# The last stage of a two-layer GNN and expert kernel: half 1's tokens scattered to places group by group, its expert results added into the output, the last tile finished beside the first expert sets

## The chip, the cores and the metric

The kernel runs on one core of one Trainium2 chip. Its time is device time in microseconds (us), of one launch that computes the whole reference. The median of several runs is the figure that is compared; the profile comes from one profiled execution of its own time.

The core's engines work side by side, each through its own instructions in order: PE (matrix multiply; PEld is its weight load), DVE and ACT (vector and activation work), POOL (here mostly transfers with indices) and SP (here only transfers). Transfers run on 16 DMA engines. Data in the on-chip memory lie in 128 partitions; "128x256" is 128 partitions of 256 elements.

## The reference, cut to what matters

There are N = 3125 tokens of D = 256 features and 50000 edges. Two layers follow each other, and each adds a graph part and an expert part to x. The second layer is the one that the change touches:

```
# layer 2, graph part (gnn): count-weighted sums over edges
t1    = feat @ W1                            # feat = layernorm(x)
msg   = t1[src] + feat[src] * feat[dst] @ W2
msg   = msg / (sqrt(deg[src]) * sqrt(deg[dst]))
embed = where(in_cnt > 0, t1 + segment_sum(msg, dst), 0) + b
embed = leaky_relu(embed, 0.01)
x     = x + embed / max(norm(embed), 1e-12)

# layer 2, expert part (ffn), tokens = layernorm(x)
probs = softmax(tokens @ router_w.T)         # 8 experts
rw, re = top_k(probs, 2); rw = rw / rw.sum()
out = tokens
for e in range(8):
    h = gelu(tokens @ w1[e] + b1[e])         # 256 -> 256
    out = out + combine[:, e] * (h @ w2[e] + b2[e])
x = x + out
```

Every token goes to its two best experts, and the result is x plus the normed tokens plus the two weighted expert outputs.

## The kernel before

**Tiles, halves, sets.** The 3125 tokens are 25 tiles of 128; the last one (tile 24) has 53. `X` holds all of x on the chip. The expert part works on two halves, tiles 0 to 13 and 14 to 24 (`HALVES`). For each half there are eight sets, one for each expert, with a fixed room of 4 tiles of 128 places in half 0 and 3 in half 1 (`UNITS`); tokens that don't fit would go to extra sets behind a branch at the end, which is not taken in the profiled execution. So sets 0 to 7 are half 0's, sets 8 to 15 half 1's.

**Aggregation.** `to_the_end` runs the end of the program. PE sums, for two tiles at a time, products of the edge counts (`at`) and the neighbours' parts (L1503). Behind the sums of each tile stands `finish_tile`: the products with the summed neighbours (L1395), four transposes (L1399), a copy by ACT (L1401), the dense matmuls (`y`, L1404), leaky ReLU and the square sum (L1406 to L1409). When a group of five tiles is complete (0 to 4, 5 to 9, 10 to 13, 14 to 18, 19 to 23, and 24 alone), `unit` divides by the norm and adds into `X` (L1417), and `score` takes the layer norm (L479 to L486, `xn`), transposes it (L815), multiplies by the router (L820) and, for half 1, writes `xn` to a table in memory, `xtab`. POOL adds `xn` to `X` (L1421).

**Routing.** `route_steps` ranks the scores of a half (L567 to L574), counts the tokens of each expert, gives each token a place, computes the two weights, and `list_steps` (L737 to L765 and beyond) turns this into lists: which token stands in which place (`take`), and which row of the result table it goes to (`put`). Half 0's routing runs in the aggregation; then `dispatch` has POOL scatter its rows (L1475) to their places in a table, two scatters for each tile. Half 1's routing (`beside_third`) runs in steps beside the first sets: `experts` has fixed points between its matmuls (`slot`), and each takes one step from the work beside it.

**Experts.** For a set, the rows come by one load of SP for half 0 (L904, places are in order in the table), and by three POOL gathers for half 1 (L909, by the list). PE transposes them (L925) and DVE copies them to `xs` (L926). PE multiplies by the first weights into `big` (L949), ACT applies GELU into `hid` (L953), PE multiplies by the second weights (`y`, L962), DVE adds the bias (L967; ten `y` buffers), and POOL scatters the 128 rows to the result table `ytab` (L968). Weights are loaded three sets ahead by SP (L844 to L852). The order on each engine is the order in which the program was written out (`manual_schedule`).

**The end.** Results of half 0 are read back beside half 1's sets (`beside_fourth`): SP loads two tiles of `ytab` (L985), DVE adds weight times result into `X` (L998), SP stores the tiles to `out` (L1015). After the last set `combine_all` does the same for half 1, with six loads in flight, the last tile's 53 rows by a load (L989) and a store (L1018) of their own. Then the branch on extra sets closes the program (L1549).

Of the kernel before, what the change touches and what calls it, by code (L numbers as in the profile page):

```python
# [40 lines left out]
UNITS = (4, 3)  # L41
FIXED = [NE * u for u in UNITS]
# [26 lines left out]
def groups(n, size, first=0):  # L69
    return [(a, min(a + size, n)) for a in range(first, n, size)]  # L70

# [18 lines left out]
def gnn_ffn_kernel(ctx: ExitStack, tc: tile.TileContext, x, src_a, src_d, dst_d, dst_row,  # L90
# [134 lines left out]
    def clear(ytab):  # L225
        for _ in clear_steps(ytab):
            pass

    def tables(h, layer, by_place=False):

        rows = (FIXED[h] + XS * SX if by_place else HALVES[h][1] - HALVES[h][0]) * P
        return (dram.tile([rows, D], F32, name=f"xtab{layer}{h}{int(by_place)}"),
                dram.tile([2 * tokens(h), D], F32, name=f"ytab{layer}{h}{int(by_place)}"))
# [343 lines left out]
    class Routed:  # L577
# [5 lines left out]
        def __init__(self, by_place=False, part=T):  # L583
            self.by_place = by_place
            self.part = part
            self.done = False
            self.lists = {}
# [26 lines left out]
    def route(*args):  # L614
        r = Routed()
        for _ in route_steps(r, *args):
            pass
        return r

    def route_steps(r, rp, h, pl, layer, sc=None):  # L620
# [87 lines left out]
        yield from list_steps(r, rp, h, layer, 0, FIXED[h])  # L708
# [17 lines left out]
        r.weight_x = keep.tile([P, 2, n], F32, tag=f"weightx{layer}{h}", name="weight_x")  # L726
        nc.vector.scalar_tensor_tensor(r.weight_x, r.at, FIXED[h] * P - 0.5, r.weight, OP.is_gt, OP.mult)
        yield

    def list_steps(r, rp, h, layer, c0, c1):  # L730

# [13 lines left out]
        pt = bank([P, 2, nl], F32, "sa", 1)  # L745
# [7 lines left out]
        for i, a, b in parts:  # L753
# [6 lines left out]
            col = rp.tile([P, min(r.part, n), 2, nl], BF16, name="col", bufs=2)  # L760
            nc.vector.tensor_tensor(in_pairs(col[:, :m, 1, :]), pairs(cb[:, i, a:b], nl),
                                    in_pairs(iota_b[:, None, :nl].to_broadcast([P, m, nl])), OP.is_equal)
            nc.vector.tensor_tensor(in_pairs(col[:, :m, 0, :]), in_pairs(col[:, :m, 1, :]),
# [20 lines left out]
        none = rp.tile([P, nl], F32, name="no")  # L784
        nc.vector.tensor_scalar(none, pt[:, 0, :], 0.5, float(1 << 20), OP.is_lt, OP.mult)
        nc.vector.tensor_tensor(put, which, none, OP.max)
        r.lists[c0, c1] = (take, put)
# [14 lines left out]
    def score(sp, h, t0, t1, pl, Wt, xtab, also=None, kept=None, queue=nc.sync):  # L802
# [3 lines left out]
        xn = kept if kept is not None else sp.tile([P, 5, D], F32, name="xn5")  # L806
        for t in range(t0, t1):
            normed(xn[:, t - t0, :], X[:, t, :], mv, t - t0)
            if also:
                also(t, xn[:, t - t0, :])  # L810
        for a, b in groups(t1 - t0, 2):
# [5 lines left out]
            nc.scalar.copy(hT[:, :b - a], pt[:, :b - a])  # L817
            for i in range(a, b):
# [3 lines left out]
        if kept is None:  # L822
            queue.dma_start(out=xtab[(t0 - first) * P:(t1 - first) * P, :].rearrange("(t p) d -> p t d", p=P),
                            in_=xn[:, :t1 - t0, :])

    def alone(dma, table, fresh=False):
# [3 lines left out]
        tc.add_to_no_dep_group(group, dma.ins)  # L830

# [23 lines left out]
    def experts(fp, sets, routed, tabs, weights, nh, act, beside=(), fresh=False, early=0, loaded=None,  # L855
# [60 lines left out]
        def turn(k):  # L916
            if k < len(sets):
# [3 lines left out]
                turned[k] = fp.tile([P, KD, max(UNITS) * P], F32, name="xs", bufs=1)  # L921
# [8 lines left out]
        with tc.manual_schedule(engines=ENGINES):  # L930
            for _ in range(early):
                slot()
# [7 lines left out]
            for k, (h, e, x) in enumerate(sets):  # L940
# [4 lines left out]
                hid = fp.tile([P, nh, max(UNITS) * P], F32, name="hid", bufs=2 if nh == 2 else 1)  # L945
# [13 lines left out]
                for j in range(n):  # L959
                    py = bank([P, D], F32, "y")  # L960
                    for c in range(nh):
# [6 lines left out]
                    alone(nc.gpsimd.indirect_dma_start(  # L968
                        out=tabs[h][1], out_offset=bass.IndirectOffsetOnAxis(ap=routed[h].column(c0 + j)[1], axis=0),
                        in_=y, in_offset=None, bounds_check=2 * tokens(h) - 1, oob_is_err=False), tabs[h][1], fresh)  # L970
# [30 lines left out]
    def combine_all(fp, h, r, ytab, over, then=lambda t0, t1: None, bufs=2):  # L1001
        spans = groups(HALVES[h][1], 2, HALVES[h][0])
        ahead = []
        for i, (t0, t1) in enumerate(spans):
            while len(ahead) < min(bufs, len(spans) - i):
                ahead.append(results(fp, h, ytab, *spans[i + len(ahead)], bufs))
            y2 = ahead.pop(0)
            for t in range(t0, t1):
                combine(h, r.weight_x if over else r.weight, y2, t0, t)
            then(t0, t1)  # L1010

    def store(t0, t1):
        whole = min(t1, T - 1)
        if whole > t0:
            nc.sync.dma_start(out=out[t0 * P:whole * P, :].rearrange("(t p) d -> p t d", p=P),  # L1015
                              in_=X[:, t0:whole, :])
        if t1 == T:
            nc.sync.dma_start(out=out[(T - 1) * P:, :], in_=X[:LAST, T - 1, :])  # L1018
# [152 lines left out]
    tabs2 = [tables(h, 2, not h) for h in range(2)]  # L1171
    routed1 = [None, Routed()]
    into = keep.tile([P, GW, W], F32)
    mv2 = keep.tile([P, T, 2], F32)
    with tc.tile_pool(name="ffn", bufs=2, reuse_waits="tile") as fp:
# [134 lines left out]
        def beside_first():  # L1310
# [7 lines left out]
            with tc.tile_pool(name="onehots", bufs=2, reuse_waits="tile") as hp:  # L1318
                yield from total_in(hp, into)
                clears = [c for table in (tabs2[0][0], tabs2[0][1], tabs2[1][1]) for c in (clear_steps(table),)]  # L1320
# [71 lines left out]
    def dense(gp, t, s, feat, some, emb, sq):  # L1392
# [3 lines left out]
        nc.vector.scalar_tensor_tensor(both[:, 1, :], s, deg[:, t:t + 1], feat, OP.mult, OP.mult)  # L1396
        pt = bank([P, 2 * KD, P], F32, "tr")
# [3 lines left out]
        nc.scalar.copy(hT, pt)  # L1401
        po = bank([P, D], F32, "y")
        for k in range(2 * KD):
            nc.tensor.matmul(po, hT[:, k, :], (hW1t if k < KD else hW2t)[:, k % KD, :],  # L1404
                             start=(k == 0), stop=(k == 2 * KD - 1))
        nc.vector.scalar_tensor_tensor(emb, po, some, hbt, OP.mult, OP.add)  # L1406
        nc.vector.scalar_tensor_tensor(emb, emb, 0.01, emb, OP.mult, OP.max)
        junk = gp.tile([P, D], F32, name="junk", bufs=1)
        nc.scalar.activation(junk, emb, AF.Square, accum_out=sq)  # L1409

    def unit(emb, sq, t0, t1):
        n = t1 - t0
        nc.scalar.activation(sq[:, :n], sq[:, :n], AF.Sqrt)
        nc.vector.tensor_scalar(sq[:, :n], sq[:, :n], 1e-12, None, OP.max)
# [7 lines left out]

    def to_the_end():


        routed2 = [Routed(True, 5), Routed()]
        with tc.tile_pool(name="ahead", bufs=6, side="right", reuse_waits="tile") as ap, \
                tc.tile_pool(name="prod", bufs=1, reuse_waits="tile") as gp:
            at = {}

            def load(t):
                if t % 8 < 6:
                    at[t] = ap.tile([P, T, P], BF16, name="at")
                else:
                    at[t] = gp.tile([P, T, P], BF16, name="at2", bufs=2)
# [10 lines left out]
            def finish_tile(sp, t, s):  # L1446
# [7 lines left out]
                dense(gp, t, s, feat, some_in[:, t:t + 1], state["emb"][:, i, :], state["sq"][:, i, :])  # L1454
                if t == t1 - 1:
                    unit(state["emb"], state["sq"], t0, t1)
                    h = int(t0 >= HALVES[1][0])
                    if t0 == HALVES[h][0]:
                        state["pl"] = bank([P, HALVES[h][1] - t0, NE], F32, "sb", 1)
                    score(sp, h, t0, t1, state["pl"], rWt, tabs2[h][0], plus_normed,  # L1460
                          state["kept"][:, t0:t1, :] if h == 0 else None, nc.scalar)
                    if h == 0 and t1 == HALVES[0][1]:
                        r = routed2[0]
                        with tc.tile_pool(name="route2", bufs=1, reuse_waits="tile") as rp:
# [330 lines left out]
```

## Time and profile before

| | us |
|---|---|
| median of 9 runs | 1171.74 (1167.44 to 1175.77) |
| the profiled execution | 1175.44 |
| its span | 1173.6 |
| PE busy in the span | 1021.9 (87%) |
| DVE busy | 589.2 (50%) |
| POOL busy | 341.9 (29%) |
| ACT busy | 323.0 (28%) |
| mean granted clock of PE | 0.922 of full speed |

The profiled execution's own time is 1.8 us above its span, and 3.7 above the median. Times in the text count from the span's start. A row of the chain of waits reads "start us, us, what"; a row of the table by stage has the window, its length, the busy time of each engine with its number of instructions, the granted clock of PE (1 is full speed), the busy share of the 16 DMA engines and the GB/s moved; a row of the waits of an engine reads "who waited <- for whom: us in total, times, longest".

### The profile page before, as it was taken

The page shows a single profiled execution, that of the slowest core. Times are in us where ns is not written, and L with a number is a line of the kernel's source. Part 1 is how long each engine was busy: PE and PEld are TensorE (multiplying, and loading weights), DVE is VectorE, ACT ScalarE, POOL GpSimd, SP SyncE. Part 2 cuts the span into 40 slices and gives each one's busy share as a digit, 9 for nine tenths or more (in the row PEclk, how much of TensorE's full clock was granted, in tenths as well). Part 3 has the DMA queues.
Part 4 walks back from the last instruction along what each step waited for, and adds up shares of the span by engine and source line. Part 5 has one row for each costly group of instructions (what it writes and reads, how often), then busy time and mean ns, then how long its engine had stood idle before and what let it go on. Part 6 is the DMA issues. An engine that isn't in the chain of part 4 may idle for free. (4 is left out here: it accounts for less than half of the span.)

```text
span 1173.6 us, 16050 instructions
## 1 busy us (share of the span) xinstructions
PE 1021.9 (87%) x6043; PEld 764.4 (65%) x6051; DVE 589.2 (50%) x1481; ACT 323.0 (28%) x709; POOL 341.9 (29%) x358
## 2 busy tenths in 40 slices
PE   6996455898999999999998999999999997888890
PEld 6884342666666677777666788878877775455560
DVE  9963394376265555656454053534371424722453
ACT  2352041121135555666432111121110112111110
POOL 1234506343332322222221111011122321256640
PEclk9887687899999999999998999999999997889895
DMA  7653344353247875786643170511122101754764
GB/s 210 216 167 111 87 163 140 111 171 124 77 120 229 288 263 212 272 291 221 224 135 118 47 292 4 225 56 57 57 84 73 46 32 50 227 163 147 230 216 158
DMA packets 116607, 179.41 MB, mean 153 GB/s; under 512 B 20204, under 2 KB 91237, under 8 KB 116393
## 3 DMA queue, kind: packets, MB, share of 16 engines
q1 hardware_dynamic: 94237, 120.40, 31.3%
q0 software_dynamic: 13296, 34.55, 9.1%
q10 hardware_dynamic: 8980, 23.26, 5.2%
q8 instruction: 51, 0.84, 0.3%
q14 instruction: 43, 0.35, 0.1%
HBM read 108.30 MB, written 71.76 MB: 153 GB/s over the span
## 5 line engine op out<-in xcount | busy, mean ns | idle before, releaser
L949 PE MATMUL big<-xs,w 128*128 128x512 f32 (+1 forms) x640 | 288.3, 576 | 17.3 <-ACT hid L953 14.9
L962 PE MATMUL y<-w,hid 128*128 128x256 f32 x1120 | 278.7, 394 | 17.7 <-issue 9.0
L962 PEld LDWEIGHTS y<-w,hid 128*128 128x128 f32 x1120 | 207.6, 195 | 48.8 <-issue 10.8
L1503 PEld LDWEIGHTS <-at 128*128 128x128 bf16 x1875 | 185.0, 99 | 29.6 <-DMA at<-atab 2.5
L968 POOL DMA_INDIRECT ytab<-y,put x112 | 123.9, 1106 | 228.1 <-DVE y L967 160.8
L953 ACT ACTIVATE hid<-big,bt 128x512 f32<-128x512 f32 (+1 forms) x160 | 101.3, 634 | 273.5 <-PE big L949 192.3
L949 PEld LDWEIGHTS big<-xs,w 128*128 128x128 f32 x640 | 116.0, 198 | 89.4 <-issue 42.7
L1503 PE MATMUL big<-parts,at 128*128 128x256 bf16 x1200 | 146.4, 275 | 2.0 <-DMA at<-atab 1.7
L909 POOL DMA_INDIRECT g<-xtab,take x80 | 81.2, 1015 | 174.3 <-PE tr L925 112.8
L967 DVE TENSOR_TENSOR y<-y,b2t 128x256 f32<-128x256 f32 x112 | 47.0, 423 | 131.2 <-PE y L962 109.0
L1160 PEld LDWEIGHTS <-hq 128*128 128x128 bf16 x800 | 57.2, 98 | 61.0 <-issue 40.6
L1140 DVE TENSOR_TENSOR hq<-qs,iota_b 128x2048 bf16<-128x2048 bf16 x50 | 61.1, 1222 | 54.3 <-PE sb L1160 48.3
L926 DVE COPY xs<-tr 128x512 f32<-128x512 f32 (+1 forms) x64 | 37.1, 618 | 80.1 <-PE tr L925 49.8
L998 DVE SCALAR_TENSOR_TENSOR X<-y,weight,X 128x256 f32<-128x256 f32 (+1 forms) x100 | 46.8, 499 | 45.2 <-DMA y<-ytab 43.7
L1503 PE MATMUL sa<-parts,at 128*128 128x256 bf16 x525 | 65.9, 277 | 1.7 <-issue 1.6
L1161 ACT CAST at<-sa 128x400 bf16<-128x400 f32 x100 | 49.1, 491 | 48.9 <-PE sa L1160 45.3
L1161 ACT CAST at<-sb 128x400 bf16<-128x400 f32 x100 | 49.0, 490 | 31.5 <-PE sb L1160 27.6
L1401 ACT COPY hT<-tr 128x512 f32<-128x512 f32 x25 | 14.4, 587 | 153.8 <-PE tr L1399 148.5
L1143 DVE TENSOR_TENSOR hc<-cs,iota_b 128x1600 bf16<-128x1600 bf16 x50 | 49.2, 984 | 0.0
L1421 POOL TENSOR_TENSOR X<-X,kept 128x256 f32<-128x256 f32 x14 | 10.4, 772 | 125.4 <-DVE kept L486 125.4
L519 PE MATMUL big<-gWo,hT 128*128 128x272 f32 x100 | 30.5, 444 | 17.8 <-remote 9.3
L417 PEld LDWEIGHTS <-hot 128*128 128x128 bf16 x391 | 40.5, 150 | 7.1 <-issue 4.0
(316 smaller groups left out, 1175.6 us busy)
## 6 DMA issues: line engine op xcount, KB each, us to landing
w<-in_fW SPq DMA_DIRECT2D x32, 1024.0 KB
atab<-at ACTq DMA_DIRECT2D x25, 800.0 KB
at<-atab SPq DMA_DIRECT2D x25, 800.0 KB
y<-ytab SPq DMA_DIRECT2D x24, 512.0 KB
ytab<-zero_b SPq DMA_DIRECT2D x10, 1024.0 KB
w<-in_mw SPq DMA_DIRECT2D x32, 256.0 KB
xtab<-zero_b SPq DMA_DIRECT2D x6, 1024.0 KB
rows<-xtab SPq DMA_DIRECT2D x8, 512.0 KB
```

The source lines that it names most:

```text
L909: nc.gpsimd.indirect_dma_start(out=g, out_offset=None, in_=tabs[h][0], in_offset=bass.IndirectOffsetOnAxis(ap=routed[h].column(c)[0], axis=0))
L949: nc.tensor.matmul(ph[:, :n * P], w1[:, i, c * P:(c + 1) * P], turned[k][:, i, :n * P], start=(i == 0), stop=(i == KD - 1))
L953: nc.scalar.activation(hid[:, c, :n * P], ph[:, :n * P], act, bias=bt[:, 0, c:c + 1])
L962: nc.tensor.matmul(py, hid[:, c, j * P:(j + 1) * P], w2[:, c, :], start=(c == 0), stop=(c == nh - 1))
L967: nc.vector.tensor_add(y, py, b2t)
L968: alone(nc.gpsimd.indirect_dma_start(out=tabs[h][1], out_offset=bass.IndirectOffsetOnAxis(ap=routed[h].column(c0 + j)[1], axis=0), in_=y, ...
L998: nc.vector.scalar_tensor_tensor(X[:n, t, :], y2[:n, t - t0, i, :], weight[:n, i, i0:i0 + 1], X[:n, t, :], OP.mult, OP.add)
L1140: nc.vector.tensor_tensor(in_pairs(hq), pairs(qs[:, mine], P), in_pairs(iota_b[:, None, :].to_broadcast([P, n, P])), OP.is_equal)
L1143: nc.vector.tensor_tensor(in_pairs(hc), pairs(cs[:, mine], C), in_pairs(iota_b[:, None, :C].to_broadcast([P, n, C])), OP.is_equal)
L1160: nc.tensor.matmul(pa[:, j], hq[:, g + j, :], hc[:, g + j, :], start=True, stop=True)
L1161: nc.scalar.copy(at[:, :, W * (g0 + g):W * (g0 + g + 4)].rearrange("p i (g w) -> p i g w", w=W), pa.rearrange("p g i w -> p i g w"))
L1503: nc.tensor.matmul(sums[a][:, t - a, :], at[t][:, i, :], parts[:, i, k, :], start=False, stop=(i == T - 1 and k == 2 and t == b - 1))
```

## The change

**Last tile.** `finish_tile`, `dense`, `unit` and `score` become generators that pause between their steps. For tiles 0 to 23 they are run through at once, as before. Tile 24's steps are the first of the work beside the expert sets (`beside_third`). The first set's `xs` and first `hid` buffer are taken ahead of the loop, and the three slots run ahead (`early=3`) fall away.

**Half 1 by place.** A new `place_steps` gives the tokens of one group their places among 24 x 128 = 3072 rows of a new table `placed`, continuing a running count for each expert (`next`), and POOL scatters them there, two scatters for each tile. It runs for tiles 14 to 18 in the aggregation, for 19 to 23 and 24 beside the first sets. The gathers of half 1's sets are replaced by SP loads, as in half 0. Instead of half 1's result table, `placed` is cleared ahead.

**Adds to the output.** For half 1, `X` plus the normed tokens is stored to `out` once a group is scored. An expert result is scaled by its weight on ACT, and POOL scatters it into `out` with an add in the transfer. The adds of one set are free of each other, and each set's follow those of the set before. `list_steps` carries the weights to the lists for this (three bfloat16 parts each, five columns in place of two), and unused places add zeros to spare rows: rows of tiles 11 to 13 of `out` (`LATE`), which are stored after all adds. The reading back, combining and storing of half 1 at the end fall away; half 0's stays, with tiles 11 to 13 stored last.

```diff
@@ list_steps
-        pt = bank([P, 2, nl], F32, "sa", 1)
+        kinds = 5 if r.adds else 2
+        if kinds > 2:
+            wb = rp.tile([P, 3, 2, n, 2], BF16, name="wb")
+            rest = r.weight
+            for k in range(3):
+                nc.vector.tensor_copy(wb[:, k], rest[:, :, :, None].to_broadcast([P, 2, n, 2]))
+                if k < 2:
+                    left = rp.tile([P, 2, n], F32, name="left", bufs=2)
+                    nc.vector.tensor_sub(left, rest, wb[:, k, :, :, 0])
+                    rest = left
+            yield
+        pt = bank([P, kinds, nl], F32, "sa", 1)
...
+            for k in range(2, kinds):
+                nc.vector.tensor_tensor(in_pairs(col[:, :m, k, :]), in_pairs(col[:, :m, 1, :]),
+                                        wb[:, k - 2, i, a:b, None, :].to_broadcast([P, m, nl // 2, 2]), OP.mult)
@@ experts
+            if nh == 2:
+                turned[0] = fp.tile([P, KD, max(UNITS) * P], F32, name="xs", bufs=1)
+                first = fp.tile([P, nh, max(UNITS) * P], F32, name="hid", bufs=2)
...
+                    to = routed[h].column(c0 + j)
+                    into = bass.IndirectOffsetOnAxis(ap=to[1], axis=0)
+                    if not routed[h].adds:
...
+                        nc.scalar.activation(y, y, AF.Identity, scale=to[2])
+                        dma = nc.gpsimd.indirect_dma_start(
+                            out=out, out_offset=into, in_=y, in_offset=None,
+                            bounds_check=N - 1, compute_op=OP.add)
+                        for group in (sums_of(h, e, x), "stores"):
+                            tc.declare_no_dep(dma.ins, group=group, reason="other rows")
+                        tc.add_to_no_dep_group(sums_of(h, e, x), dma.ins)
@@ finish_steps
+                xn = yield from score_steps(sp, h, t0, t1, state["pl"], rWt, tabs2[h][0], plus_normed,
+                                            state["kept"][:, t0:t1, :] if h == 0 else None, queue)
+                if h == 1:
+                    due.append((t0, t1, xn))
+                    list(store(t0, t1, queue))
@@ place_steps (new)
+                yield from rank_steps(rp, rank, score_, 0, n)
...
+                pp = bank([P, 2, NE, n], F32, "tr")
+                nc.tensor.matmul(pp[:, 0], upper_b, selb, start=True, stop=True)
+                nc.tensor.matmul(pp[:, 1], all_b, selb, start=True, stop=True)
+                yield
+                place = rp.tile([P, NE, n], F32, name="place")
+                for i in range(n):
+                    nc.vector.tensor_add(place[:, :, i], pp[:, 0, :, i], state["next"])
+                    nc.vector.tensor_add(state["next"], state["next"], pp[:, 1, :, i])
...
+                for t in range(n):
+                    yield
+                    for i in range(2):
+                        alone(nc.gpsimd.indirect_dma_start(
+                            out=placed, in_=xn[:, t, :], in_offset=None,
+                            out_offset=bass.IndirectOffsetOnAxis(ap=toi[:, i, t:t + 1], axis=0),
+                            bounds_check=FIXED[1] * P - 1, oob_is_err=False), placed)
@@ to_the_end
+                        if t == T - 1:
+                            last = sums[a][:, 0, :]
+                            continue
+                        run(finish_steps(t, sums[a][:, t - a, :]))
+                        if due and t < T - 2:
+                            with tc.tile_pool(name="place", bufs=1, reuse_waits="tile") as rp:
+                                run(place_steps(rp, *due.pop()))
...
+        def beside_third():
+            yield from finish_steps(T - 1, last)
+            with tc.tile_pool(name="place", bufs=1, reuse_waits="tile") as rp:
+                for one in due:
+                    yield from place_steps(rp, *one)
+            finishing.close()
+            with tc.tile_pool(name="route3", bufs=1, reuse_waits="tile") as rp:
+                yield from route_steps(routed2[1], rp, 1, state["pl"], 2)
...
-            experts(fp, fixed(0) + fixed(1), routed2, tabs2, weights2, KD, AF.Gelu,
-                    [beside_third(), beside_fourth()], early=3, now=now2, room=24)
+        experts(fp, fixed(0) + fixed(1), routed2, [tabs2[0], (placed, None)], weights2, KD, AF.Gelu,
+                [beside_third(), beside_fourth()], now=now2)
+        list(store(LATE, HALVES[0][1], nc.sync))
...
-            with tc.tile_pool(name="last", bufs=1, reuse_waits="tile") as lp:
-                combine_all(lp, 1, routed2[1], tabs2[1][1], False, store, 6)
```

In the new file's numbering the row load is L953, `xs` L976, the add L1031 and its scaling on ACT just ahead of it.

## The prediction

> **What bounds the kernel now.** I read the page's slices first, then a table of busy time by stage over the last 200 us, then the chain of waits in order of time, then SP's own waits. The table by stage of the part that the change touches:
>
> ```profile
> ...
> core 0: us, PE busy (x) PEld busy (x) DVE busy (x) ACT busy (x) POOL busy (x), PEclk, DMA share, GB/s
> ...
> 980.00:1000.00 20.00, 11.66 (x45) 8.93 (x44) 7.35 (x21) 5.62 (x11) 1.81 (x3) 0.52 0.31 96
> 1000.00:1020.00 20.00, 17.43 (x69) 10.34 (x70) 15.80 (x58) 2.80 (x5) 4.08 (x4) 0.88 0.85 268
> 1020.00:1087.00 67.00, 55.25 (x205) 36.27 (x205) 21.85 (x56) 8.25 (x12) 41.11 (x42) 0.90 0.48 150
> 1087.00:1144.60 57.60, 50.97 (x207) 36.51 (x205) 29.32 (x68) 9.30 (x16) 32.51 (x33) 0.94 0.68 225
> 1144.60:1173.60 29.00, 0.00 (x0) 0.00 (x0) 9.45 (x23) 0.00 (x0) 1.97 (x2) 0.56 0.47 160
> ...
> ```
>
> The aggregation before 980 is PE at work (324.65 of the 340 us from 640 to 980). Then come three places where PE is not the limit: a hole at 980 to 1000, half-clocked; sets 0 and 1 at 1000 to 1020, where DVE is busy 15.80 of 20; and 29 us without any PE at the end. The chain says what fills them:
>
> ```profile
> ...
> 976.88 2.93 DVE xn L486 x5
> ...
> 985.15 3.80 PE y L1404 x8
> ...
> 999.31 0.61 DVE xs L926
> 999.96 6.04 PE big L949 x8
> ...
> 1011.62 0.88 POOL ytab L968
> ...
> 1012.97 3.81 DMA ytab<-y,put
> ...
> 1023.00 3.43 PE big L949 x8
> ...
> 1030.93 3.43 PE big L949 x8
> ...
> 1132.05 0.66 POOL ytab L968
> ...
> 1137.88 0.66 POOL ytab L968
> ...
> 1143.56 0.16 POOL ytab L968
> ...
> 1144.84 0.62 POOL ytab L968
> ...
> 1146.13 2.31 DMA ytab<-y,put
> 1148.45 0.37 SPq L985
> ...
> 1152.79 10.73 DMA y<-ytab
> 1163.61 0.49 DVE X L998
> ...
> ```
>
> ```profile
> ...
> SPq L904 <- DVE X L1417: 38.7, 1, 38.7
> ...
> SPq L985 <- DMA ytab<-y,put: 20.2, 1, 20.2
> ...
> ```
>
> The reader sees set 0 begin at 999.96, behind tile 24's own dense, norm and score steps, and SP's load of set 0's rows (L904) held until tile 24's X. A half-0 set takes 7.93 us undisturbed (1023.00 to 1030.93), a half-1 set 5.83 (its first scatters at 1132.05 and 1137.88). At the end the last scatter lands 2.31 after its issue, the results are read back, of which the load of the last 53 rows alone takes 10.73, then combined and stored; the timeline has the last store at 1164.63, and 8.97 us of branches and closing waits follow it.
>
> **The change, part by part.** All terms are against this execution, 1175.44 us (span 1173.6). It lies 3.7 above the median of 1171.74, so I take 3.7 off at the end.
>
> *Front.* Set 0's transposes and matmuls no longer stand behind tile 24. In the new order PE does the transposes of xn of tiles 19 to 23, their score matmuls, set 0's row transposes, then L949's successor; xn ends at 979.81, the scores in the old trace at 983.30, the row transposes and two DVE copies (0.61 each) add some 2. I put the start at 985.5 in place of 999.96: −14.5. It needs set 0's rows by then: the load is now issued without a wait for tile 24, since its buffer and the first hidden tile are taken ahead; the last dispatch scatter was issued at 950.5. Tile 24's chain does not vanish: 0.53 transposes, y L1404 (3.80 at half clock, 1.9 at full), 0.34 and 0.52 for the scores at full clock, together +3.3 on PE inside sets 0 to 2. Its DVE and ACT steps (0.2 to 0.5 each) hide if PE has other matmuls between them, which the order gives; without that cover the 15 us return.
>
> PEclk is 0.52 in the hole, and set 0's eight matmuls take 6.04 where set 1's and 2's take 3.43. PE's wait for xn (up to 980) stays, so set 0 starts at a low clock again and I count none of the 2.6, with ends 0 and −2.6. The Trainium skill, "TensorE: Matmul & The Clock Gate", Part 1, says the same in a sharper form: an idle window of about 3.4 us halves the clock and a busy one restores it, which leaves the term at 0; a sum with a warm set 0 would be 2.6 lower.
>
> *Routing and places.* Half 1's scatter to places adds three runs of place_steps: some 40 small DVE operations each for tiles 14 to 18 and 19 to 23 and 30 for tile 24, two small matmuls each, 22 POOL scatters; the list gains the weight splits and 12 products. The first run lies in the aggregation, where DVE is busy 134.30 of 340: about 9 us, hidden, but PE's two matmuls stand in PE's queue behind it: +1, ends 0 and +3. The others stand beside sets 0 to 5. Small dependent DVE operations come 0.2 to 0.28 apart in the old routing (timeline from 1002 to 1016); about 150 of them and some 6 us of wide ones give 42 us, against 24 before in sets 0 and 1. In 1020 to 1087 DVE is 33% busy, so six sets of 7.93 leave 31 us; the overrun is 11. Before, two sets left 10.6 for the 20 us that fell in them, an overrun of 9, and cost 23.04 − 15.9 − 2.6 = 4.5. The same half gives 5.5 after: +1.5 for the sum (1.0 rounded up for the latency of more steps), ends −4.5 (all hides) and +6.5 (the whole overrun shows).
>
> *POOL and loads.* 24 gathers at 0.99 leave POOL's queue, 22 place scatters at 1.29 spacing enter it, 12 of them between the scatters of sets 1 to 3. Behind a place scatter that waits for DVE are set 1's to 3's result scatters, and behind these the ten y buffers, two and a half sets deep: 0, up to one set (8) if that cover is gone. Half 1's rows come by SP loads three sets ahead: 0. The early stores of base rows wait for POOL's X, and SP's 53-row store has weight loads of later sets queued behind it, which are also ahead: 0. The 24 ACT scalings are priced by ACT's 0.69 for a 128x512 tile at most, 2.1 per set, where ACT is busy 9.30 of 57.60: 0, except once in the tail.
>
> *The adds.* Each set's first scatter-add now waits on POOL until the three of the set before have landed; queued behind it are only later adds and, through the ten y buffers, PE's sets three ahead. Scatters follow at 1.29 (1143.56, 1144.84, 1146.13), so a set's period is 2.57 plus one landing, against 5.83 on PE. Plain landings: 2.31 in quiet (DMA share 0.47), 5.16 at share 0.85 (issued 1011.62, landed 1016.78). Half 1's stage has 0.68; linear between gives 3.9. No accumulating DMA stands in this trace. It must also read its target: below, nothing extra; above, a whole second quiet landing, 2.31. A 512 KB load took 4.98 from its issue at 1148.45 to the combine at 1153.43, so 128 KB more cost (4.98 − 2.31)/3 = 0.9, and I take that, being the row for more bytes in one request: landing 4.8, period 7.37, 1.54 late per set, over seven steps +10.8. Ends: 0 (landing under 3.26) and 7 × (2.57 + 5.16 + 2.31 − 5.83) = 29.5.
>
> The Trainium skill, "DMA: Bandwidth & Descriptors", Rules for kernel authors, speaks against this part: an accumulating DMA next to another access of the same bytes has to wait for that one's semaphore, so the wait can't be left away. Its section on the anatomy of one DMA has a fixed cost of about 2.0 us and 436 GB/s, an estimated 2.3 for 128 KB, which would make the period 4.9 and this term 0, and the sum −23.4.
>
> *Tail.* PE's end to the last scatter's issue is 1.58 (1144.55 to 1146.13); ACT's scaling adds 0.5, the landing 2.31 + 0.9, the last store is issued, and the same 8.97 follow, in which its 384 KB land. That is 14.3 for 29.05: −14.7, ends −15.6 (no extra read) and −11.9 (a landing of 5.16). Gone are six loads, 22 combines and six stores. What is late next is the closing branch of SP.
>
> Sum: −14.5 + 3.3 + 1 + 1.5 + 10.8 − 14.7 = −12.6, so 1162.8 for this execution and 1159 for the median.
>
> **The rivals.** *No lag:* the adds land in under 3.26 and hide behind PE: −12.6 − 10.8 = −23.4, 1148. For it: the last scatters of the trace land in 2.31. Against: DMA is at 320 to 390 GB/s from 1102 to 1127, and every add reads too.
>
> *Slower, the adds bound half 1:* with the target read as a second full round, landing 7.47, the lag is 29.5 and the change ends at −12.6 + 18.7 = +6.1, 1178. It decides from a lag of 26.9 (for +3.5), that is 3.84 per set, a landing of 7.1. For it: 5.16 is there without the read. Against: only the part of half 1 beside the read-back of half 0 is loaded.
>
> *The front doesn't move:* set 0's rows load, or PE's queue, still ends behind tile 24's chain, because a step of it that stands between the first matmuls waits for DVE or ACT. Then 14.5 are lost and the time is +1.9, 1174. For it: PE is in order and DVE is the fuller engine there. Against: in the new order only tile 24's four transposes stand inside set 0's first matmuls, and these need one feature and two products (0.4 each).
>
> **How the numbers follow.** Forecast (lag 5 to 16) 0.42, no lag 0.26, adds bound 0.17, front unmoved or DVE crowding as much 0.15. The forecast's own range is 1153 to 1165. A measurement of this kernel tells about 0.3%, 3.5 us, from no change. Faster: 0.42 + 0.26 + 0.04 of the last = 0.72; same 0.06; slower 0.17 + 0.05 = 0.22. The range runs from the no-lag case with DVE's low end (1144) to a little over the slower rival (1179).
>
> **What would show it.** Right: the first big matmul of set 0 near 985; eight half-1 sets on PE still 5.8 apart, and the adds' first issues about 7.4 apart, POOL waiting on its own landings; no DVE combines after PE's end; the last store followed by 9 us. Wrong: adds 5.8 apart (no lag) or over 9.7 (slower); PE waiting for tile 24's hT or X inside sets 0 and 1; DVE above 90% busy in sets 1 to 5; PE stopped for y buffers.

## The result and the profile after

The changed kernel is slower by 1.9%: 1194.74 us median (1187.16 to 1200.3, 10 runs) against 1172.67 for the kernel before in the same rounds, ratio 1.0188 (1.0161 to 1.0214). Forecast was 1159, with a range up to 1179. The profiled execution took 1196.55, its span is 1194.8, 21.2 above the one before.

The table by stage, cut where the stages now end (the last sums, set 0's first matmul, half 1's first, PE's end):

```profile
...
core 0: us, PE busy (x) PEld busy (x) DVE busy (x) ACT busy (x) POOL busy (x), PEclk, DMA share, GB/s
998.80:1007.90 9.10, 7.23 (x39) 6.33 (x39) 3.82 (x7) 2.99 (x5) 3.70 (x5) 0.70 0.86 276
1007.90:1102.50 94.60, 75.57 (x301) 50.02 (x301) 56.19 (x199) 18.16 (x27) 42.31 (x43) 0.87 0.54 172
1102.50:1158.60 56.10, 48.92 (x203) 35.02 (x202) 29.26 (x66) 20.54 (x39) 26.03 (x18) 0.97 0.85 230
1158.60:1194.80 36.20, 0.00 (x0) 0.00 (x0) 0.42 (x1) 0.67 (x2) 13.97 (x9) 0.56 0.35 49
...
```

The same cuts of the two traces, in us (the aggregation's own length runs from its first to its last matmul):

| stage | before | after | difference |
|---|---|---|---|
| start of the aggregation's matmuls | 675.8 | 673.9 | −1.9 |
| aggregation | 300.6 | 324.9 | +24.3 |
| last sums to set 0 | 23.6 | 9.1 | −14.5 |
| half 0's sets | 87.9 | 94.6 | +6.7 |
| half 1's sets, to PE's end | 56.6 | 56.1 | −0.5 |
| PE's end to the span's end | 29.1 | 36.2 | +7.1 |

So the front came in as forecast, and two things overturned it: the aggregation, which should have been 1 longer, and the end, which should have been shorter. Within the aggregation it is one stretch:

```profile
...
945.00:955.00 10.00, 9.90 (x72) 8.32 (x71) 3.62 (x10) 2.19 (x6) 7.56 (x9) 1.00 0.27 98
955.00:976.00 21.00, 7.91 (x30) 2.59 (x28) 0.00 (x0) 0.00 (x0) 13.25 (x14) 0.58 0.23 91
976.00:998.00 22.00, 21.91 (x167) 18.36 (x167) 7.33 (x22) 2.40 (x7) 0.00 (x0) 0.94 0.00 1
...
```

From 955 to 976 PE does 30 matmuls where the 22 us behind hold 167. DVE and ACT do nothing (here they may only lack PE's sums), the DMA engines are a quarter busy, and only POOL works. The timelines of PE and of POOL there (start, length, engine, line, operation, out<-in, count, and the idle time ahead with what ended it):

```profile
...
971.38 0.37 PE L1656 MATMUL big<-parts,at 128*128 128x256 bf16 x1 [1.73 <-issue]
...
975.61 9.71 PE L1656 MATMUL big<-parts,at 128*128 128x256 bf16 x74 [0.35 <-issue]
...
```

```profile
...
944.31 0.99 POOL L1629 DMA_INDIRECT xtab<-kept,place  x1 [10.82 <-DVE place L1626]
945.60 0.99 POOL L1618 DMA_INDIRECT placed<-xn,toi  x1 [0.30 <-DVE both L1458]
...
957.19 0.98 POOL L1618 DMA_INDIRECT placed<-xn,toi  x1 [0.30 <-issue]
958.47 0.97 POOL L1629 DMA_INDIRECT xtab<-kept,place  x1 [0.30 <-issue]
...
971.23 0.97 POOL L1629 DMA_INDIRECT xtab<-kept,place  x1 [0.30 <-issue]
...
```

PE waits for nothing that the profile names ("issue"), does one to three matmuls at a time, and is back at full pace some 3 us after POOL's last scatter. POOL issued 22 scatters without a gap from 944.3 to 972.2. Before, half 0's dispatch scatters (now L1629) went out four to eight at a time, the last at 950.5. Now eleven of them stand in POOL's queue behind the ten place scatters, and these had to wait for DVE's place steps, which DVE ended at 944.2 (the places as whole numbers, `toi`):

```profile
...
943.99 0.17 DVE L1614 CAST toi<-to 128x10 int32<-128x10 f32 x1
...
```

The same shows beside the sets: POOL has a train of 16 from 1035.1 to 1055.8, and PE stands from 1044.9 to 1058.3. In the waits from 1040 to 1062 that reads:

```profile
...
PE y L1016 <- DVE y L1021: 13.5, 1, 13.5
DVE xs L976 <- remote: 6.2, 1, 6.2
...
```

PE's wait is put down to DVE, whose bias adds (L1021) make room for PE's next `y`, but DVE stands as well, for something that the profile doesn't name ("remote"): its second copy to `xs` had its transposes by 1043 and began only at 1052.2, though DVE did nothing from 1046 on. The chain of waits is of no use here, it ends in one piece, the last add. At the end of the kernel POOL's timeline shows the adds:

```profile
...
1111.85 1.55 POOL L1031 DMA_INDIRECT out<-y,put  x1 [0.30 <-ACT hid L1007]
1120.97 1.54 POOL L1031 DMA_INDIRECT out<-y,put  x1 [7.58 <-DMA out<-y,put]
...
1172.12 1.55 POOL L1031 DMA_INDIRECT out<-y,put  x1 [0.30 <-issue]
1176.64 1.55 POOL L1031 DMA_INDIRECT out<-y,put  x1 [2.96 <-DMA out<-y,put]
...
1180.35 1.55 POOL L1031 DMA_INDIRECT out<-y,put  x1 [0.30 <-issue]
```

An add occupies POOL 1.55 (a scatter: 0.97), and adds follow at 1.86. A set's first add comes 4.5 after the last one of the set before in quiet, 9.1 under load. The sets' adds are 12.9, 11.2 and 11.2 apart at first and 8.2 to 8.5 later, where PE needs 5.8. The last add is issued 21.8 after PE's end.

### The profile page after: what moved, and what is told of

Same layout as the page of the kernel before. It is cut to its first block, busy times and chain, and to the rows that moved or that the text cites. A ratio compares the mean times of both kernels' runs of the same rounds, so it can differ in the third digit from the quotient of the medians.

```text
span 1194.8 us, 16193 instructions
## 1 busy us (share of the span) xinstructions
PE 1025.2 (86%) x6049; PEld 764.1 (64%) x6057; DVE 599.3 (50%) x1559; ACT 337.6 (28%) x736; POOL 353.9 (30%) x360
## 3 DMA queue, kind: packets, MB, share of 16 engines
q0 software_dynamic: 15504, 34.55, 10.1%
## 5 line engine op out<-in xcount | busy, mean ns | idle before, releaser
L1003 PE MATMUL big<-xs,w 128*128 128x512 f32 (+1 forms) x640 | 292.1, 581 | 14.9 <-ACT hid L1007 12.9
L1016 PE MATMUL y<-w,hid 128*128 128x256 f32 x1120 | 273.0, 389 | 23.8 <-DVE y L1021 23.6
L1016 PEld LDWEIGHTS y<-w,hid 128*128 128x128 f32 x1120 | 204.5, 192 | 51.3 <-DVE y L1021 26.9
L1656 PE MATMUL big<-parts,at 128*128 128x256 bf16 x1200 | 157.2, 283 | 15.2 <-issue 13.1
L1025 POOL DMA_INDIRECT ytab<-y,put x88 | 99.2, 1127 | 216.2 <-DVE y L1021 149.3
L958 POOL DMA_INDIRECT g<-xtab,take x56 | 57.4, 1025 | 167.4 <-PE tr L975 112.8
L1021 DVE TENSOR_TENSOR y<-y,b2t 128x256 f32<-128x256 f32 x112 | 47.0, 422 | 116.8 <-PE y L1016 95.1
L976 DVE COPY xs<-tr 128x512 f32<-128x512 f32 (+1 forms) x64 | 37.2, 618 | 67.9 <-PE tr L975 58.3
L1064 DVE SCALAR_TENSOR_TENSOR X<-y,weight,X 128x256 f32<-128x256 f32 (+1 forms) x78 | 37.9, 505 | 41.2 <-DMA y<-ytab 38.2
L1457 DVE SCALAR_TENSOR_TENSOR both<-big,deg,feat 128x256 f32<-128x256 f32 x16 | 7.7, 478 | 86.0 <-PE big L1656 85.9
L1031 POOL DMA_INDIRECT out<-y,put x24 | 37.4, 1560 | 38.8 <-DMA out<-y,put 16.7
```

What stands on the lines that cost most here:

```text
L958: nc.gpsimd.indirect_dma_start(out=g, out_offset=None, in_=tabs[h][0], in_offset=bass.IndirectOffsetOnAxis(ap=routed[h].column(c)[0], axis=0))
L1003: nc.tensor.matmul(ph[:, :n * P], w1[:, i, c * P:(c + 1) * P], turned[k][:, i, :n * P], start=(i == 0), stop=(i == KD - 1))
L1016: nc.tensor.matmul(py, hid[:, c, j * P:(j + 1) * P], w2[:, c, :], start=(c == 0), stop=(c == nh - 1))
L1021: nc.vector.tensor_add(y, py, b2t)
L1025: alone(nc.gpsimd.indirect_dma_start(out=tabs[h][1], out_offset=into, in_=y, in_offset=None, bounds_check=2 * tokens(h) - 1, oob_is_err=Fa ...
L1064: nc.vector.scalar_tensor_tensor(X[:n, t, :], y2[:n, t - t0, i, :], weight[:n, i, i0:i0 + 1], X[:n, t, :], OP.mult, OP.add)
```

## The experiments

Two theories. *Trains:* an unbroken row of POOL's indexed transfers stops the other engines, from about its tenth until shortly after its last. *Adds:* accumulating scatters that wait for each other set by set fix the pace of half 1. The rivals: the new order of PE's and DVE's work delays the aggregation, and any scatter would land as late. The kernel before had medians from 1164.86 to 1172.12 in the rounds of these runs, so runs of different rounds are compared by their ratios.

**One train, nothing else changed.** In the kernel before, the scatters of half 0's tiles 4 to 13 are issued together:

```diff
-                            if 0 <= first < HALVES[0][1]:
+                            if 0 <= first < 4:
                                 dispatch(first, first + 2)
+                            if t == HALVES[1][0] + 6:
+                                dispatch(4, HALVES[0][1])
```

> The kernel before, with one move only: the dispatch scatters of half 0's tiles 4 to 13, issued in groups of four behind tiles 16 to 20, all stand behind tile 20, so that POOL issues 20 of them without a gap; no work is added. Train theory (an unbroken train of some 15 or more of POOL's indexed transfers slows the other engines from about 10 us after its start to about 2.5 us after its end): the train lasts 20 x 1.28 = 25.6 us, so PE should crawl for some 15 to 18 us in the aggregation, its sums should end at about 990 to 994 in place of 976.4, and the time should be 12 to 18 us longer than before (ratio 1.010 to 1.015). Rival (PE's crawl after the change came from the new order of its own work or of DVE's place steps): PE's sums still end within 2 us of 976.4 and the time is that of before within 0.3%.

Measured: 1188.26 (before 1172.12), ratio 1.0171 (1.0127 to 1.0214). The train ran from 939.5 to 964.8, the aggregation took 310.6. By stretches:

```profile
...
940.00:952.00 12.00, 9.98 (x84) 8.28 (x82) 0.91 (x2) 0.51 (x2) 9.26 (x10) 1.00 0.28 100
952.00:968.00 16.00, 5.25 (x19) 1.89 (x20) 0.00 (x0) 0.00 (x0) 9.78 (x11) 0.59 0.25 90
...
```

The same picture as after the change, with no place steps and no added work: 19 matmuls in 16 us while POOL issues its last eleven scatters. That the train does it is shown. The two profiled executions differ by 10.3 (1185.74 and 1175.44), and the aggregation has 10.0 of that. The medians differ by 16 because this profile lies 2.5 under its median and the one of before 3.3 above the median of these rounds.

**Two trains of ten.** The same, with `dispatch(4, 9)` behind tile 18 and `dispatch(9, 14)` behind tile 20.

> The kernel before with the same 20 dispatch scatters of half 0's tiles 4 to 13 as in the single train, but ten of them behind tile 18 and ten behind tile 20, some 10 us apart or more; no work is added. Train theory by its length: PE crawled from about 12 us after a train's start, and a train of ten lasts 12.8, so each costs PE 1 to 3 us; PE's sums of the aggregation take 301 to 306 us (before 300.6, one train of 20: 310.6) and the time is 0 to 6 us above before. Rival (what counts is that the scatters are bunched or late at all, not the unbroken length): the time is within 4 us of the single train's, 12 to 20 above before.

Measured: 1169.62 (before 1164.86), ratio 1.0048 (1.0021 to 1.0075); the aggregation took 303.1, with one gap of PE of 3.3 and one of 1.6, each at the very end of a train (928.1 and 950.2, trains until 929.1 and 950.8). The aggregation's length alone would not show it: in three runs below that have it written alike (the front alone and its two runs with breaks) it took 295.3 to 300.9. The gaps and the ratio do: length is what counts, not bunching.

**Half the rows.** The single train with 64 rows in each scatter (`kept[:64]`, `place[:64]`).

> The kernel before with the single train of 20 dispatch scatters behind tile 20, each of only 64 of the 128 rows, so that half of the rows of tiles 4 to 13 are missing in the table; half the bytes and rows, as many instructions. If the crawl hangs on the rows or bytes in flight (a ring or a queue that fills): it starts after 18 or more scatters or not at all, and the aggregation takes 300 to 304 us, the time within 5 us of before. If it hangs on the number of transfers or on POOL's time in them: it starts again about 9 scatters after the train's start, and the aggregation takes 306 to 311, unless POOL issues them faster, in which case the train ends sooner and the loss shrinks with it.

Measured: 1183.85 (before 1164.86), ratio 1.0167 (1.0135 to 1.0198). POOL needs 0.90 in place of 0.97 for half the rows.

```profile
...
946.00:964.00 18.00, 4.57 (x18) 1.41 (x15) 0.00 (x0) 0.00 (x0) 11.36 (x13) 0.61 0.22 49
...
```

Half the bytes (49 GB/s for 90), and the crawl starts again behind the eighth scatter and costs no less: the aggregation took 315.2. It hangs on the number of transfers or on POOL's time in them, not on bytes or rows.

**Small operations in the train.** POOL operations were written behind every sixth scatter of the single train.

> The kernel before with the single train of 20 dispatch scatters behind tile 20, now with six small POOL operations (iota into a scratch tile, some 1.5 us together) behind every sixth scatter. If only an unbroken row of transfers hurts, and a gap of 1 to 2 us starts the count anew: the crawl goes, the aggregation's matmuls take 300 to 304 us (single train 310.6), the time is within 5 us of before. If the count runs on over such a gap, or the number of transfers in some 25 us is what matters: the crawl starts again behind the ninth or tenth scatter, the aggregation takes 308 to 315 and the time is 12 us or more above before.

Measured: 1179.74 (before 1167.02), ratio 1.0116 (1.0062 to 1.017). It tells nothing on breaks: this part of the program isn't written out in order, and in the trace the 20 scatters still follow at 1.28 from 932.4 to 957.5. It repeats the train instead, with 313.4 in the aggregation.

**The place steps moved.** In the changed kernel, place steps of tiles 14 to 18 behind tile 21, after all of dispatch:

```diff
-                        if due and t < T - 2:
-                            ... run(place_steps(rp, *due.pop()))
                         first = 2 * (t - HALVES[1][0])
                         if 0 <= first < HALVES[0][1]:
                             dispatch(first, first + 2)
+                        if due and t == T - 4:
+                            ... run(place_steps(rp, *due.pop()))
```

> The changed kernel with the place steps of tiles 14 to 18 run behind tile 21 in place of tile 18, so that all of half 0's dispatch scatters are ahead of them, as in the kernel before, and the ten place scatters stand alone; same work. Train theory: the train of 22 scatters at 944 to 972 becomes groups of four to ten, PE's crawl at 955 to 976 goes, its sums end at about 979 to 983 in place of 998.8, set 0 starts at about 988 to 992 in place of 1007.9, and the time falls by 14 to 19 us against the change. Rival (the place steps as such delay the aggregation): the sums end within 5 us of 998.8 again.

Measured: 1183.05 (before 1172.12), ratio 1.0114 (1.0053 to 1.0174), 11.7 under the change and short of the 14 to 19 expected. The aggregation took 313.2 and set 0 started at 992.6, 8.2 behind the sums. A train of 14 was left (943.0 to 960.6, the ten joined by the last four of dispatch), and PE crawled from 955 to 961.5. One tile later (`t == T - 3`) the ten stand alone:

> The changed kernel with the place steps of tiles 14 to 18 behind tile 22, one tile later than in the run with tile 21, so that the ten place scatters no longer join the last dispatch group to a train of 14; same work. Train theory: PE's crawl of 955 to 961.5 goes, the aggregation's matmuls take 304 to 308 us in place of 313.2 (behind tile 21) and 324.9 (behind tile 18); what is left over the 300.6 of before is the routing of half 0 in smaller parts, where PE waits 3 to 5 us for DVE; time 3 to 8 us under the tile-21 run, 1175 to 1180. Rival (place steps delay the sums wherever they stand): 312 or more again.

Measured: 1177.04 (before 1164.86), ratio 1.0122 (1.0073 to 1.0172); the aggregation took 298.7, no more than the 300.6 of before. The place steps as such cost it nothing that shows, and my estimate of 3 to 5 us for half 0's routing in smaller parts was wrong too. But the timed runs show nothing of it: the ratio is 1.0122 beside 1.0114, from four runs each. At the next step the last group's norm shares its buffer with the rows that POOL was still scattering until 975.2, so PE stood from 969.4 to 977.4, and set 0 began 16.5 behind the sums in place of 8.2; that is more than half of what the aggregation won (14.5).

**Breaks beside the sets.** That kernel, with ten small POOL operations behind every sixth scatter beside half 0's sets; there the order is fixed, and they landed where they were written.

> The changed kernel with the place steps of tiles 14 to 18 behind tile 22, and ten small POOL operations (some 1.5 us) behind every sixth scatter beside the half-0 sets. Theory that the 10 to 13 us stall of PE in set 3 comes from POOL's train of 16 to 17 (result scatters and twelve place scatters): the stall shrinks to below 4 us, half 0's sets take 82 to 88 us in place of 93.4, and the time is 5 to 10 us below that run, at 1168 to 1173. Rival (the stall is POOL being behind with the result scatters, so that the ten y buffers run out): the stall stays or grows, since POOL has more to do.

Measured: 1166.92 (before 1167.02), ratio 1.000 (0.9968 to 1.0032); half 0's sets took 83.3 in place of 93.4. The stretch of the stall without and with breaks:

```profile
...
1015.00:1038.00 23.00, 10.38 (x39) 6.56 (x38) 10.23 (x36) 2.94 (x4) 15.68 (x16) 0.76 0.45 157
...
```

```profile
...
1015.00:1038.00 23.00, 18.87 (x71) 11.64 (x69) 17.60 (x71) 5.48 (x7) 15.05 (x32) 0.93 0.56 181
...
```

71 matmuls for 39, although POOL had more to do; one pause of 3.5 is left. The y buffers running out would have grown worse. So it is the unbroken row of transfers that counts and not POOL being busy. With the trains broken or apart the whole change comes to nothing, neither gain nor loss.

**The add taken out.** The changed kernel without `compute_op=OP.add`.

> The changed kernel with the add taken out of the scatter (plain scatter to the same rows of the output, same order, same waits), so half 1's output rows hold the last scattered product only. Theory that the add itself is dear: a scatter takes POOL 0.97 again and follows at 1.29 in place of 1.55 and 1.86, its landing falls from about 4.6 to 2.3 in quiet, a set's period to 5.8 (PE's own), PE's waits for the y buffers at 1119 to 1138 (6.9 in all) vanish, and the span from PE's end to the last landing falls from 27 to about 5: 25 to 30 us less than the change, 1165 to 1170. Rival (the chain of waits from set to set costs what it does with any scatter, since the landing under load is long): the period stays above 8 and the time within 8 us of the change.

Measured: 1178.65 (before 1172.12), ratio 1.0069 (1.0037 to 1.0101): 16 under the change, between the theory's 25 to 30 and the rival's 8. Its adds' timeline, first under load, then in quiet:

```profile
...
1116.49 0.98 POOL L1031 DMA_INDIRECT out<-y,put  x1 [0.30 <-ACT hid L1007]
1125.03 0.98 POOL L1031 DMA_INDIRECT out<-y,put  x1 [7.56 <-DMA out<-y,put]
...
1158.65 0.98 POOL L1031 DMA_INDIRECT out<-y,put  x1 [0.30 <-issue]
1162.38 0.98 POOL L1031 DMA_INDIRECT out<-y,put  x1 [2.75 <-ACT y L1030]
...
1164.96 0.98 POOL L1031 DMA_INDIRECT out<-y,put  x1 [0.30 <-issue]
1169.91 0.98 POOL L1031 DMA_INDIRECT out<-y,put  x1 [3.96 <-DMA out<-y,put]
...
```

In quiet the plain scatters mostly keep PE's pace (the sets' first ones are 5.9 and 6.3 apart). The last set's had to wait for a plain landing of 5.0 (1164.96 to 1169.91), though, as long as an add's 4.5, so a quiet landing of a plain scatter isn't always the 2.31 of before. Under load it lands 8.5 later, hardly better than the add's 9.1: there it is the load and not the add. PE's end to the span's end fell from 36.2 to 23.8. What the add costs the DMA engines shows where little else runs; POOL's queue in the changed kernel (1158 to 1182, nine adds) and in this one (1147 to 1162, six scatters), as packets, MB and share of 16 engines:

```profile
...
q0 software_dynamic: 1251, 1.13, 42.3%
...
```

```profile
...
q0 software_dynamic: 351, 0.94, 15.7%
...
```

Per MB that is 24 x 0.423 / 1.13 = 9.0 us of all engines against 15 x 0.157 / 0.94 = 2.5. The adds' bytes also go in smaller packets, 0.9 KB on average against 2.7.

**Two tables.** Half 1's odd experts add to a second table, so a set waits for the one two before.

```diff
-                            out=out, out_offset=into, in_=y, in_offset=None,
+                            out=aside if h == 1 and x is None and e % 2 else out, ...
```

> The changed kernel with the adds of half 1's odd experts going to a second table in memory (cleared ahead with four further transfers), so that a set waits for the set two before and not for the last one; the odd experts' share is then missing from the output. Theory that the wait from set to set sets the pace: two chains of about 8.3 each run side by side, the adds come at PE's pace of 5.8 per set (POOL itself needs 3 x 1.86 = 5.6), PE's waits for y buffers go, and the last landing follows PE's end by about 6 to 8 in place of 27: 22 to 28 us less than the change. Rival (the DMA engines or POOL can carry no more adds than this): the period stays above 7.5 and at most 8 us come back.

Measured: 1178.13 (before 1172.12), ratio 1.0067 (1.0034 to 1.01), 16.6 under the change where the theory had 22 to 28. PE's end to the span's end fell from 36.2 to 19.3, the last add was issued 3.2 after PE's end in place of 21.8; half 1's sets took 59.5, still with waits of PE of 1.9 to 3.5 under load, where most sets' adds stay 8.2 to 9.7 apart; behind it they are 5.7 to 5.8 apart, PE's pace. So the wait from set to set cost 17 us at the end, of which half 1's sets took back 3.4. Without it these sets and the end together are 6.9 shorter than in the kernel before (78.8 for 85.7).

**The front alone.** Tile 24 beside the first sets, as in the change, but no places and no adds: half 1 gathers, scatters to its table, and is combined at the end as before.

> One part of the change alone: tile 24's chain stands beside the first sets and the first set's buffers are taken ahead, while half 1 keeps its gathers, its result table, and the reading back, combining and storing at the end (the last tile's normed rows share the buffer of the group before). Theory (front gain real, 14.5 us from the last sums to set 0 as in the change; the loss came from the places' trains and the adds): the sums end at about 976 to 979, set 0 starts 9 to 10 us later, half 0's sets take 88 to 92, and the time falls by 8 to 14 us against before. Rival (what the front gains is lost again in the sets, to tile 24's work on PE and DVE and to POOL's trains of scatters and gathers): the time is within 4 us of before.

Measured: 1152.98 (before 1164.86), ratio 0.9901 (0.9868 to 0.9935). It beats both kernels, the one before by 1.0% (four runs). The last sums end at 967.2 after 300.2 in the aggregation, set 0 starts at 975.9, 8.7 later. Its halves:

```profile
...
975.90:1061.60 85.70, 71.89 (x297) 46.80 (x297) 43.95 (x133) 18.27 (x27) 41.02 (x42) 0.96 0.56 172
1061.60:1122.20 60.60, 51.72 (x203) 35.55 (x202) 29.40 (x67) 9.30 (x16) 37.20 (x38) 0.94 0.65 225
...
```

**The front with breaks.** The three pauses that PE has beside the sets, before and here, lie at the end of POOL's trains of 10 to 14 scatters and gathers. So I broke these, first behind every sixth transfer:

> The front part alone (tile 24 beside the first sets, half 1 gathered and combined as before) with the same small POOL operations behind every sixth of the sets' scatters and gathers. Before, and with the front alone, POOL's trains of 13, 14 and 10 are each followed by a pause of PE (2 to 4 us, then half clock). If a gap restarts the count: these pauses go and 4 to 10 us come off the front run's time, some 1143 to 1149 where before is 1165. If it does not: POOL, which is nearly full in half 0, falls behind by up to 80/6 x 1.5 = 20 us spread over the sets, and the time is equal or up to 8 us above that of the front alone.

Measured: 1164.18 (before 1167.02), ratio 0.9975 (0.9947 to 1.0003). Half 0 took 78.3 in place of 85.7, and none of the pauses at the end of a train is left in it; but half 1 took 72.2 in place of 60.6, since POOL was behind and the read-back of half 0 waited for it, with DVE's queue behind that (DVE's timeline):

```profile
...
1079.81 3.75 DVE L1077 SCALAR_TENSOR_TENSOR X<-y,weight,X 128x256 f32<-128x256 f32 x8 [8.23 <-DMA y<-ytab]
...
```

Then behind every eighth, in half 0 only, with the first combine one set later:

> The front part alone with six small POOL operations (1.6 us) behind every eighth of POOL's transfers, in half 0's sets only, and the first combine of half 0's results one set later. With a break behind every sixth transfer half 0 took 78.3 us in place of 85.7, but POOL was behind when half 1 began, DVE stood 8.2 us before the first combine, and half 1 took 72.2 in place of 60.6. If that is the whole of it: trains stay at eight or less in half 0, half 0 takes 78 to 82, half 1 58 to 64, and the time is 4 to 10 us below that of the front alone, 0.98 to 0.986 of before. Rival (POOL, with 80 transfers at 1.29 and the breaks, has no room: what the breaks save is paid back as late scatters and gathers): half 1 takes 66 or more and the ratio is 0.988 or above.

Measured: 1168.02 (before 1171.11), ratio 0.996 (0.9939 to 0.998). Half 0 took 79.3, half 1 68.8, with a train of 16 from 1079.5 to 1099.8 and PE standing from 1092.4 to 1101.4. The rival holds: POOL has no room for the breaks with 80 transfers in these sets, and what they save comes back later.

## Why the prediction was wrong

**The step that failed** is the term for the places in the aggregation, "+1, ends 0 and +3". It priced DVE's steps and PE's two matmuls and left out what the step does to POOL's queue: dispatch stood behind ten scatters that wait for DVE, and 22 went out as one train. Measured: +24.3, and 298.7 in place of 324.9 with the same steps four tiles later. The same blind spot is in the step on POOL beside the sets: I gave it 0, "up to one set (8) if that cover is gone", by the y buffers. PE stood 13.5 behind the train of 16 there, and breaking such a train gave back 10.1 in half 0. Half 0's sets were only 6.7 longer, since the kernel before had pauses of its own there, 4.1 and 3.6 at the end of two trains of 14; a third, of 1.6 and 2.9 at the end of a train of 12, lies in half 1. These pauses stood in the trace of before, unexplained, and I left them out of the sum.

**The adds** were the right mechanism with a mis-sized term: +10.8, measured about 19.7 (21.8 from PE's end to the last issue, less 1.6 and the 0.5 of ACT). Counted as the term counts, by the period, it is 27.7: the sets' first adds are 9.8 apart on average (68.6 over seven steps), 3.96 more than PE's 5.83. The part of it that doesn't show behind PE's end lies ahead of it: PE itself stood 6.9 for `y` buffers. Three sizes were low. POOL's spacing of 1.29 became 1.86, so three adds take 3.7 and not 2.6 before the landing; the trace had no row for it. The quiet landing was set at 3.2 and came out as 4.0 (1180.35 to the store at 1184.32), near the upper bound of 4.6. And I interpolated the load with half 1's mean DMA share of 0.68, where the sets that matter run at 0.95 (1104 to 1148). The closing behind the last store was not the same 8.97 either, but 10.5.

**What held.** The front: 9.1 for 23.6, −14.5 as forecast, and PE's clock there is 0.70, not yet restored. The sets' +4.8 for tile 24 and DVE was not what failed: the front alone, with tile 24's work, has half 0 at 85.7, and the run with breaks beside the sets, with the place steps too, at 83.3, both shorter than the 87.9 before. The end without lag did not quite hold: forecast 14.3, and two tables, the nearest to it, gave 19.3.

**The rivals.** The one on the slower side named the adds' chain and a landing of 7.1; under load it was 9.1, in quiet 4.0, so the chain took back more than the 14.7 that the tail should bring. By its own sign, adds over 9.7 apart, it came true (9.8), as did PE stopped for `y` buffers. But it wouldn't have made the kernel slower without the trains: with these broken or apart the ratio was 1.000. "The front doesn't move" is refuted. The train was on no list, and with it the range was too low by 16.

## What to carry to other kernels

Count the indexed transfers that GpSimd issues in a row without a gap: here rows of four left no such gap, rows of eight gaps of 1.4 to 3.4, two rows of ten 3.3 and 1.6, one of 20 cost some 10 to 16 us, and a pause of "issue" or "remote" on several engines at once near the end of such a row is its sign. When a step with scatters is put ahead of others in that queue, ask what it holds back and whether it will come out as one row. Scatter-adds that must wait for each other are worth it only where a landing, priced under the load of that stage and not the kernel's mean, fits into the time of the work between them.

## What the runs showed of the hardware

- A long row of back-to-back indexed transfers of POOL slowed or stopped PE, mostly from its seventh to tenth transfer, until 1 to 4 us after its last, with half as many rows as well; beside the sets DVE and ACT stood too (6.2 "remote" and 5.6 "issue" in the train of 16). Breaks of some 2 to 3 us behind every sixth took most of it away there. What the engines share isn't shown: between 955 and 976 the DMA engines were a quarter busy.
- An accumulating scatter of 128 rows of 1 KB takes POOL 1.55 in place of 0.97, and the DMA engines 3.6 times as long per MB (9.0 and 2.5); in quiet the next work could start 4.0 to 4.8 after its issue, where plain ones landed in 2.31 before and in 2.55 and 5.0 in the run without the add.
- The Trainium skill, "DMA: Bandwidth & Descriptors", has a fixed cost of about 2.0 us for a DMA (Anatomy of one DMA). The plain scatters' 2.31 and 2.55 in quiet agree; the plain one of 5.0, the adds' 4.0 to 4.8, and 8.5 to 9.1 for either kind under load (a DMA share of 0.95 and more), don't follow from it.
